# Expert lists cut to their likely length with the rest in runtime branches, and a new order and mix for the last layer

## The chip, the core and the metric

The kernel runs on one core of one Trainium2 chip. The metric is the device time of one execution in microseconds. Five engines work side by side and wait for each other by semaphores: TensorE (PE; its weight loads are shown as PEld), VectorE (DVE), ScalarE (ACT), GpSimd (POOL) and SyncE (SP). SP issues the plain transfers here, POOL the indirect ones, whose addresses are read from a table of row numbers.

## The reference

A model of four layers on x of shape [4, 1024, 128] in float32. Each layer is a token mixer and a feed-forward part, and after each of the eight a layer norm without gain:

```python
x = layernorm(x + L0_attn(x)); x = layernorm(x + L0_ffn(x))
x = layernorm(x + L1_attn(x)); x = layernorm(x + L1_ffn(x))   # 16 experts, 4 a token, and a shared one
x = layernorm(x + L2_attn(x)); x = layernorm(x + L2_ffn(x))   # 8 experts, 2 a token
x = layernorm(x + L3_attn(x)); x = layernorm(x + L3_ffn(x))   # 32 experts, 4 a token, and a shared one
```

The mixer of layer 3 is the one that the change touches. Its sequence axis is the axis of length 4 (the rows), so that the Toeplitz mix runs over four positions with seven coefficients a head:

```python
rms = norm(query, axis=-1) * 128 ** -0.5
x = query / (rms + 1e-8)
u = silu(x @ u_w.T + u_b);  v = silu(x @ v_w.T + v_b)          # 256 features each
y[i] = sum over j of toeplitz[i - j] * v[j]                    # i, j: the four rows
L3_attn = (u * y) @ o_w.T + o_b + query
```

A routed feed-forward part computes, for each token, the softmax or sigmoid of its router's logits, takes the best k experts, and adds their outputs with weights. An expert of layers 1 and 3 is `(silu(x @ gate) * (x @ up)) @ down` with 128 hidden units; one of layer 2 has 512 and low-rank additions.

## The kernel before

**Tokens and tiles.** The 4096 tokens lie in SBUF as `self.x`, 32 tiles of 128 tokens by 128 features. A quarter is 256 time steps of the four rows, 8 tiles. A `Part` is a set of tiles that goes through a stage together. In layer 1 part a has quarters 0 and 1, r quarters 2 and 3. In layer 2 part a has the same two quarters, m has rows 0 and 1 of quarters 2 and 3, n has their rows 2 and 3. In layer 3 part a has quarters 0 and 1, b quarter 2, c quarter 3.

**A routed part.** `positions` (L1231 to 1291) computes on VectorE and TensorE where each token's copies stand in a list that is sorted by expert, each expert's share padded to whole tiles of 128 rows. It leaves a table of row numbers `pos`, the weights `wk` and `ids`, the expert of each tile. `spread` (L1307, its transfers recorded at L1295) has POOL scatter the rows of x into a list in DRAM, one indirect transfer for each tile and choice. The list has room for the worst padding: the number of tiles times k, plus one for each expert, in whole groups of four: 80 tiles for layer 1's parts, 40, 24 and 24 for layer 2's a, m and n, 96, 64 and 64 for layer 3's a, b and c. Lists are zeroed at the start by SP (`zero_lists`, L1343).

**Experts.** `small_experts` (L1663; layers 1 and 3) and `l2_experts` (L1440) walk the whole list in groups of four tiles: `inputs` loads a group by SP and transposes it, `up` multiplies by gate and up, `turn` transposes the product, `down` multiplies by down, and SP stores the result into a second list, ys. Each group's experts are read from `ids` into registers of the engines (L1337). When the last group is issued, the name "made ..." goes into `self.listed`. `collect` (L1350) then has POOL gather k rows for each token from ys into a tile `yt`, and VectorE adds them into x with their weights (L1361). A gather waits for a free `yt`; in layer 3 the pool `yp` has 8 of them, each for one tile's four gathers.

**Layer 3's mixer.** `l3_attn` (L1512) works quarter by quarter: norm of 8 tiles (L185, applied on VectorE at L205), the root mean square by squares and sums (L1548, L1549), scaling, twice the input plus the bias put back into x (L1564), transposes, projections to u and v with `silu`, the mix over the rows, the output matmul and its sum with x, and a second norm. The mix is on VectorE: for each of 2 feature chunks and 4 rows one product (L1590), three multiply-adds (L1592) and a product with u (L1594 or L1596). With `exps` (part a) ScalarE is kept to the table that the layer-2 softmax uses; parts b and c go without.

**The order.** Every stage is a Python generator; what it issues between two `yield`s is a step. `mix(main, side, pace)` (L233) interleaves a main generator and a side one by the costs that the steps yield, written by hand. `abreast` (L1772) runs generators in turn, `chain` one after the other, `when` waits until a name is in `listed`, `press` runs the side until a condition holds. From the parts of layer 2 on, one side chain `on` runs through all stages (L1858 to 1887). Its last piece has, in order: the collection of n's rows, the mixer and routing of b, then b's scatter and `last(a, yp)` (64 gathers of a and its final norm) abreast with the mixer and routing of c, then c's scatter, and `last(b, yp)`. The main generators beside it are the shared expert and the experts of a, b and c. At the end `close(c, yp)` collects c. `last` (L1809) is `collect` and `finish` (L1738), which norms and stores the output.

After all that, one branch on `flag` (L1891, 1892) guards a general version of layer 2 and what follows, for inputs that overflow the fast softmax; with these inputs it isn't run.

Of the kernel before, what the change touches and what calls it, by code (L numbers as in the profile page):

```python
# [12 lines left out]
I32 = mybir.dt.int32  # L13
# [61 lines left out]
class Kernel:  # L75
# [109 lines left out]
    def norm(self, tiles, by="act"):  # L185

        nc, n = self.nc, len(tiles)
        mv = self.tile(self.small, [P, n, 2], f"mv{n}")
        for t, x in enumerate(tiles):
            st = self.tile(self.small, [P, 6], "bn")  # L190
            nc.vector.bn_stats(st, x)  # L191
            nc.vector.bn_aggr(mv[:, t, :], st)
        rstd = self.tile(self.small, [P, n], f"rstd{n}")
        if by == "act":
            nc.scalar.activation(rstd, mv[:, :, 1], AF.Sqrt, bias=self.eps)
            nc.vector.reciprocal(rstd, rstd)
        else:
            ve = self.tile(self.small, [P, n], f"ve{n}")
            nc.vector.tensor_scalar(ve, mv[:, :, 1], LN_EPS, None, ALU.add)
            if by == "pool":  # L200
                nc.gpsimd.tensor_tensor(rstd, ve, self.mhalf[:, :n], ALU.pow)
            else:
                self.rsqrt(rstd, ve)
        for t, x in enumerate(tiles):
            nc.vector.tensor_scalar(x, x, mv[:, t, 0:1], rstd[:, t : t + 1], ALU.subtract, ALU.mult)  # L205
# [1025 lines left out]
    def positions(self, cp, name, mask, w, nt, ne, k):  # L1231
# [51 lines left out]
        nc.vector.tensor_copy(ids, pe[0:1, :P])  # L1283

# [6 lines left out]
        self.route[name] = [pos, wk, ids, []]  # L1291
# [15 lines left out]
    def spread(self, lay, part, k):  # L1307

        pos, _, _, done = self.route[lay + part.name]
# [32 lines left out]

    def zero_lists(self, *lays):  # L1343

        for rows, _, tl in (v for k, v in self.lists.items() if k[0] in lays):
            self.nc.sync.dma_start(
                out=rows.rearrange("(t p) d -> p t d", p=P), in_=self.zero.unsqueeze(1).to_broadcast([P, tl, D])
            )

    def collect(self, lay, part, k, yp, first=0, nt=None):  # L1350

        nc = self.nc
        pos, wk, _, _ = self.route[lay + part.name]
# [12 lines left out]
        for t in range(first, first + (nt or part.nt)):  # L1366
# [73 lines left out]
    def l2_experts(self, part, wall):  # L1440
        nc = self.nc
        NC, EW = F2 // P, 3 * F2
        pos, wk, ids, done = self.route["l2" + part.name]
        rows, ys, tl = self.lists["l2", part.name]
        with ExitStack() as ctx:
# [47 lines left out]


# [3 lines left out]
            for n in range(tl + 1):  # L1498
# [8 lines left out]
                if n == tl:  # L1507
                    self.listed.add("made l2" + part.name)
# [3 lines left out]
    def l3_attn(self, part, exps=False):  # L1512
# [5 lines left out]
        with ExitStack() as ctx:  # L1518
# [19 lines left out]
            for q in range(part.q0, part.q0 + part.nq):  # L1538
                s = slice(q * QT, (q + 1) * QT)
                self.norm(self.quarter(q), by="dve" if exps else "act")  # L1540
                yield (7.0,)
                xq = self.tile(vp, [P, QC], "xq")
                rms = self.tile(self.small, [P, QT], "rms")
                for g in range(2):
                    sg = slice(q * QT + g * 4, q * QT + g * 4 + 4)
                    r = rms[:, g * 4 : g * 4 + 4]
                    sq = self.tile(vp, [P, 4, D], "sq")
                    nc.vector.tensor_tensor(sq, x[:, sg, :], x[:, sg, :], ALU.mult)  # L1548
                    nc.vector.tensor_reduce(r, sq, AX.X, ALU.add)  # L1549
                    if exps:  # L1550

                        ri = self.tile(self.small, [P, 4], "rmsi")
                        v = self.tile(self.small, [P, 4], "rmsv")
                        nc.vector.tensor_scalar(v, r, 1e-30, None, ALU.max)
                        self.rsqrt(ri, v)
                        nc.vector.tensor_tensor(r, r, ri, ALU.mult)
                    else:
                        nc.scalar.activation(r, r, AF.Sqrt)
                    nc.vector.tensor_scalar(r, r, float(np.float32(D ** -0.5)), 1e-8, ALU.mult, ALU.add)
                    nc.vector.reciprocal(r, r)  # L1560
                    yield (4.0,)
                    nc.vector.tensor_tensor(sq, x[:, sg, :], r.unsqueeze(2).to_broadcast([P, 4, D]), ALU.mult)

                    stt(  # L1564
                        x[:, sg, :], x[:, sg, :], 2.0, self.row["l3_ob"].unsqueeze(1).to_broadcast([P, 4, D]),
                        ALU.mult, ALU.add,
                    )
# [6 lines left out]
                for c in range(NC):  # L1574
                    v = self.tile(vp, [P, B, TQ], "v")
                    for i, dst in ((1, v), (0, u[:, c])):
                        for g in range(2):
# [3 lines left out]
                            yield (2.3,)  # L1581

                    cf = col["toep"][:, c * 7 : (c + 1) * 7]
                    for i in range(B):
                        y = self.tile(vp, [P, TQ], "y", bufs=1 if exps else 2)
# [7 lines left out]
                        if exps:  # L1593
                            stt(u[:, c, i, :], u[:, c, i, :], 0.25, y, ALU.mult, ALU.mult)  # L1594
                        else:
                            nc.vector.tensor_tensor(u[:, c, i, :], u[:, c, i, :], y, ALU.mult)  # L1596
                        yield (3.0,)
                for g in range(2):
                    py = self.tile(ps, [P, 4, D], "s")
                    for k in range(4):  # L1600
                        b, h = (g * 4 + k) // 2, k % 2
                        for c in range(NC):
                            self.mm(py[:, k, :], u[:, c, b, h * P : (h + 1) * P], wo[:, c, :], c == 0, c == NC - 1)
                    sg = slice(q * QT + g * 4, q * QT + g * 4 + 4)
                    nc.vector.tensor_tensor(x[:, sg, :], py, x[:, sg, :], ALU.add)
                    yield (3.0,)
                self.norm(self.quarter(q), by="dve" if exps else "act")
# [4 lines left out]


# [49 lines left out]
    def small_experts(self, lay, ne, part, wall):  # L1663

        nc = self.nc
        pos, wk, ids, done = self.route[lay + part.name]
        rows, ys, tl = self.lists[lay, part.name]
        with ExitStack() as ctx:
# [46 lines left out]


# [3 lines left out]
            for g in range(ng + 1):  # L1720
# [7 lines left out]
                if g == ng:  # L1728
                    self.listed.add(f"made {lay}{part.name}")
# [8 lines left out]
    def finish(self, part):  # L1738

        for q in range(part.q0, part.q0 + part.nq):  # L1740
            self.norm(self.quarter(q))
            yield (5.0,)
            for b in range(B):
                t = tile_of(b, 2 * q)
                self.nc.sync.dma_start(
                    out=self.out[b, q * TQ : (q + 1) * TQ, :].rearrange("(k p) d -> p k d", p=P),
                    in_=self.x[:, t : t + 2, :],
                )
            yield (1.0,)
# [59 lines left out]
    def last(self, part, yp):  # L1809
        yield from self.collect("l3", part, K3, yp)  # L1810
        yield from self.finish(part)
# [12 lines left out]
    def all(self):  # L1824
# [4 lines left out]
        with ExitStack() as ctx:  # L1829
# [36 lines left out]
            with ExitStack() as c3:  # L1866
                with ExitStack() as c2:
# [5 lines left out]
                    on = self.chain(on, self.rows_in(m2))  # L1873
                    self.run(self.mix(self.l2_experts(n2, wall), on, drain=False))
                self.press(on, listed("l3a"))
                yp = self.pool(c3, "l3y", 8)
                on = self.chain(
                    on, self.rows_in(n2), self.l3_attn(b), self.l3_route(b),
                    self.abreast(
                        self.chain(self.spread("l3", b, K3), self.when(listed("made l3a")), self.last(a, yp)),  # L1880
                        self.chain(self.l3_attn(c), self.l3_route(c)),
                    ),
                    self.spread("l3", c, K3), self.when(listed("made l3b")), self.last(b, yp),
# [8 lines left out]
        with self.tc.If(bad > 0):  # L1892
            with ExitStack() as ctx:
# [4 lines left out]
                for p in self.by_rows:  # L1898
# [3 lines left out]
                    self.run(self.rows_in(p))  # L1902
                for p in self.parts:
                    self.run(self.onward(p))
                    with ExitStack() as c2:
                        sw, wall = self.l3_wall(c2)
                        self.run(self.l3_shared(p, sw), self.l3_experts(p, wall))
                        self.run(self.last(p, self.pool(c2, "l3y" + p.name, 5)))
# [165 lines left out]
```

## Time and profile before

| what | us |
|---|---|
| median of three runs | 2526.44 (2516.18 to 2534.73) |
| the profiled execution | 2521.14 |
| its span | 2519.3 |

Where the stages of the last third stand in the profiled execution, by the instructions that open or close them:

| us from the start | what |
|---|---|
| 1720 to 1767 | experts of m (layer 2) on TensorE |
| 1787.3 | positions of a (layer 3) are there |
| 1788 to 1874 | POOL scatters a |
| 1943.5 | last experts of n (layer 2) |
| 1989 to 2102 | experts of a, with b's mixer and routing beside them |
| 2106.6 | positions of b |
| 2107 to 2148, 2148 to 2190 | POOL scatters b, gathers the first half of a's |
| 2205 to 2335 | experts of b |
| 2277.6 | positions of c |
| 2284 to 2326, 2338 to 2378 | POOL scatters c, gathers b's |
| 2385 to 2461 | experts of c |
| 2465 to 2505 | POOL gathers c's |
| 2519.3 | end |

The profile page gives, for each engine, its busy time as a share of the span; the span cut in 40 slices of 63 us with a digit for each; the chain of work that ended last; and groups of equal instructions. A group's line reads: line of the kernel, engine, operation, output tile <- input tiles, count, busy time in us, mean in ns, then the idle time before it and what ended that. Three groups of the mixer, for all calls of its kind:

```profile
L205 DVE TENSOR_SCALAR x<-x,mv,rstd 128x128 f32<-128x128 f32 x256 | 71.9, 354 | 4.0 <-POOL rstd L201 3.1
...
L1592 DVE SCALAR_TENSOR_TENSOR y<-v,ld,y 128x256 f32<-128x256 f32 x96 | 43.7, 480 | 7.1 <-ACT v L1531 5.6
...
L1590 DVE TENSOR_SCALAR y<-v,ld 128x256 f32<-128x256 f32 x32 | 10.5, 345 | 22.5 <-issue 22.4
```

96 instructions of the multiply-add took 43.7 us in all, 480 ns each, and VectorE sat idle 7.1 us before them.

### The profile page before, as it was taken

The numbers are of one execution on the slowest core, as the hardware profiler recorded it, in microseconds if no ns is written. First come the engines' busy times: TensorE is split into PE (matmuls) and PEld (weight loads), VectorE is DVE, ScalarE is ACT, GpSimd is POOL, SyncE is SP. The second block draws the span as 40 slices with busy tenths as digits, with TensorE's granted clock in tenths as the row PEclk, the third lists the DMA queues.
The fourth block names the chain that finished last, engine by engine and source line by source line (L and its number), as shares of the span: only waits on it lengthen the run. The fifth ranks groups of instructions, "written<-read, shape, count | busy, mean of one in ns | idle before, by whom it ended". The sixth has DMA issues, their size and how long they took to land.

```text
span 2519.3 us, 28678 instructions
## 1 busy us (share of the span) xinstructions
PE 1708.3 (68%) x9605; PEld 1036.4 (41%) x9605; DVE 1344.4 (53%) x3801; ACT 828.6 (33%) x1193; POOL 767.0 (30%) x701
## 2 busy tenths in 40 slices
PE   7535775985652864887888778978718896374490
PEld 3224333853320444755523232345415684163280
DVE  8857894656551643334536664654603575163363
ACT  5510471432320431222246554622202353131140
POOL 5521384136145004213231002001470204536404
PEclk9756788998775987898979898988958998587695
DMA  9900002334100032312210000030410232132242
GB/s 308 289 2 0 16 34 87 118 130 164 48 30 37 27 126 93 106 48 60 89 48 16 1 1 18 1 128 32 168 65 23 74 114 72 40 108 81 63 126 60
DMA packets 225735, 192.05 MB, mean 76 GB/s; under 512 B 17008, under 2 KB 204272, under 8 KB 225072
## 3 DMA queue, kind: packets, MB, share of 16 engines
q1 hardware_dynamic: 204880, 147.28, 18.4%
q0 software_dynamic: 20704, 42.86, 5.4%
q8 instruction: 83, 1.36, 0.2%
q14 instruction: 68, 0.56, 0.1%
HBM read 93.47 MB, written 96.60 MB: 75 GB/s over the span
## 4 chain that ended last, share of the span: by engine, by line
PE 36%; another core or an unknown queue 18%; DVE 14%; issue 4%; ACT 3%; POOL 2%; DMA 2%; SPq 0%; DVEq 0%; POOLq 0%; ACTq 0%
PE gu L157 10%; PE s L157 8%; PE sc L157 5%; PE yp L157 5%; PE tp L165 4%; ACT pr L1051 1%; DVE pr L1057 1%; POOL yt L1295 1%; DVE x L205 1%; PE pu L157 1%; PE py L157 1%; PE pg L157 1%; DVE x L1361 1%; DVE bn L191 1%
## 5 line engine op out<-in xcount | busy, mean ns | idle before, releaser
L1051 ACT ACTIVATE pr<-sc 128x1024 f32<-128x1024 f32 x288 | 279.6, 1021 | 326.3 <-PE sc L157 205.8
L157 PE MATMUL gu<-ld,xgT 128*128 x768 | 203.2, 408 | 69.0 <-ACT xgT L167 40.7
L157 PE MATMUL sc<-qm,kT 32*128 32x512 f32 (+3 forms) x1536 | 202.1, 566 | 11.9 <-ACT pr L1051 8.9
L157 PE MATMUL s<-pr,va 128*32 128x512 f32 (+3 forms) x1536 | 179.2, 537 | 44.7 <-issue 26.9
L157 PEld LDWEIGHTS gu<-ld,xgT 128*128 128x128 f32 x768 | 145.7, 201 | 98.3 <-ACT xgT L167 45.2
L165 PE MATMUL tp<-ld,hg 128*128 128x128 f32 x736 | 120.0, 286 | 94.1 <-issue 46.9
L157 PE MATMUL gu<-wall,xgT 128*128 x352 | 180.7, 639 | 2.8 <-ACT xgT L167 2.0
L169 DVE COPY hT<-tp 128x512 f32<-128x512 f32 x140 | 95.8, 685 | 128.4 <-PE tp L165 61.4
L165 PEld LDWEIGHTS tp<-ld,hg 128*128 128x128 f32 x736 | 95.2, 147 | 153.9 <-issue 86.2
L1693 DVE TENSOR_TENSOR hg<-sg,gu 128x256 f32<-128x256 f32 x192 | 78.7, 416 | 138.9 <-ACT sg L1692 117.9
L1057 DVE TENSOR_TENSOR pr<-pr,ld 128x512 f32<-128x512 f32 (+1 forms) x160 | 92.4, 580 | 104.4 <-ACT pr L1051 102.1
L1692 ACT ACTIVATE sg<-gu 128x256 f32<-128x256 f32 x192 | 72.7, 383 | 209.8 <-PE gu L157 97.2
L167 ACT COPY xgT<-tp 128x512 f32<-128x512 f32 x118 | 69.0, 586 | 201.3 <-PE tp L165 152.4
L157 PEld LDWEIGHTS sc<-qm,kT 32*128 32x128 f32 x1536 | 86.1, 199 | 118.2 <-issue 69.2
L1466 ACT ACTIVATE sg<-gu 128x512 f32<-128x512 f32 x88 | 52.4, 598 | 238.1 <-PE gu L157 136.2
L165 PE MATMUL tp<-ld,xg 128*128 128x128 f32 x472 | 78.7, 294 | 52.4 <-ACT hT L167 29.5
L1295 POOL DMA_INDIRECT l1ra<-x,posl1a x64 | 93.3, 1458 | 61.2 <-DVE posl1a L1272 42.0
L157 PE MATMUL yp<-ld,hT 128*128 x768 | 105.3, 281 | 4.1 <-issue 1.9
L1468 DVE TENSOR_TENSOR hg<-sg,gu 128x512 f32<-128x512 f32 x88 | 59.9, 681 | 88.1 <-ACT sg L1466 75.1
L1295 POOL DMA_INDIRECT yt<-l1yr,posl1r x64 | 60.7, 949 | 146.7 <-DVE x L1361 72.2
L157 PEld LDWEIGHTS s<-pr,va 128*32 128x32 f32 x1536 | 38.5, 113 | 154.5 <-issue 106.7
L157 PE MATMUL yp<-wall,hT 128*128 x704 | 98.3, 286 | 1.5 <-DVE hT L169 1.5
(433 smaller groups left out, 3543.4 us busy)
## 6 DMA issues: line engine op xcount, KB each, us to landing
wall<-wall SPq DMA_DIRECT2D x16, 768.0 KB
l3ra<-zero SPq DMA_DIRECT2D x1, 6144.0 KB
ld<-in_l_w SPq DMA_DIRECT2D x2, 3072.0 KB
wall<-we SPq DMA_DIRECT2D x24, 256.0 KB
ld<-in_l_w SPq DMA_DIRECT2D x1, 6144.0 KB
xg<-l3ra SPq DMA_DIRECT2D x24, 256.0 KB
l3ya<-yg SPq DMA_DIRECT2D x24, 256.0 KB
l1ra<-zero SPq DMA_DIRECT2D x1, 5120.0 KB
```

What stands on the lines that cost most here:

```text
L157: return self.nc.tensor.matmul(out, lhsT, rhs, start=start, stop=stop)
L165: nc.tensor.transpose(pt[:, k * P : (k + 1) * P], s, self.ident)
L167: nc.scalar.copy(dst, pt[:, : n * P])
L169: nc.vector.tensor_copy(dst, pt[:, : n * P])
L191: nc.vector.bn_stats(st, x)
L1051: nc.scalar.activation(pr, sc[h], AF.Exp)
L1057: nc.vector.tensor_tensor(d, d, cst["tril"].unsqueeze(1).unsqueeze(1).to_broadcast([P, 2, n, P]), ALU.mult)
L1295: ins = self.nc.gpsimd.indirect_dma_start(**kw)
L1466: nc.scalar.activation(sg, gu[:, 0, :], AF.Silu)
L1468: nc.vector.tensor_tensor(h, sg, gu[:, 1, :], ALU.mult)
L1692: nc.scalar.activation(sg, pg[:, :, 0, :], AF.Silu)
L1693: nc.vector.tensor_tensor(h[:, 2 * c : 2 * c + 2, :], sg, pg[:, :, 1, :], ALU.mult)
```

## The change

**Lists.** A new function `likely` gives a shorter length for each list (the tiles times k plus half the number of experts, in whole groups). The expert loops end there. What lies beyond, up to the full length, is put into a branch that every engine takes or skips by a count, `used`, which `positions` now also copies out. `zero_lists` also zeroes the part of ys that lies beyond.

```diff
+        used = self.tile(self.routes, [1, 1], f"used{name}", I32)
+        nc.vector.tensor_copy(used, end[0:1, ne - 1 : ne])
...
+    def likely(self, part, ne, k):
+        return -(-(part.nt * k + ne // 2) // 4) * 4
+
+    def rest_of(self, used, at, tl, body):
+        if at >= tl:
+            return
+        n = self.nc.values_load(used, min_val=0, max_val=tl, skip_runtime_bounds_check_because="a list's tiles")
+        with self.tc.If(n > at):
+            for g in range(at // 4, tl // 4):
+                body(g)
...
-        rows, ys, tl = self.lists[lay, part.name]
+        rows, ys, total = self.lists[lay, part.name]
+        tl = self.likely(part, ne, K3)
...
+            def rest(g):
+                inputs(g)
+                up(g)
+                turn(g)
+                down(g)
...
                 if g == ng:
+                    self.rest_of(used, tl, total, rest)
                     self.listed.add(f"made {lay}{part.name}")
```

The lengths become 72 and 72 (of 80) in layer 1, 36 (of 40), 20 and 20 (of 24) in layer 2, 80 (of 96), 48 and 48 (of 64) in layer 3.

**Layer 3's mixer.** The root mean square comes from the norm's own variance. The output bias is a matmul of one row into the output's PSUM tile. For b and c (no `exps`) the norm is applied on ScalarE, and the mix is a matmul with 14 diagonal matrices (7 coefficients, 2 chunks), made once by `l3_mixes`.

```diff
         for t, x in enumerate(tiles):
-            nc.vector.tensor_scalar(x, x, mv[:, t, 0:1], rstd[:, t : t + 1], ALU.subtract, ALU.mult)
+            if on_act:
+                nc.scalar.activation(x, x, AF.Identity, bias=off[:, t : t + 1], scale=rstd[:, t : t + 1])
+            else:
+                nc.vector.tensor_scalar(x, x, mv[:, t, 0:1], rstd[:, t : t + 1], ALU.subtract, ALU.mult)
...
-                    nc.vector.tensor_tensor(sq, x[:, sg, :], x[:, sg, :], ALU.mult)
-                    nc.vector.tensor_reduce(r, sq, AX.X, ALU.add)
...
-                    stt(
-                        x[:, sg, :], x[:, sg, :], 2.0, self.row["l3_ob"].unsqueeze(1).to_broadcast([P, 4, D]),
-                        ALU.mult, ALU.add,
-                    )
...
+                    if not exps:
+
+                        for i0 in range(0, B, 2):
+                            y = self.tile(ps, [P, 2, TQ], "s")
+                            lags = [0, -1, -2, -3, 1] if i0 == 0 else [0, 1, 2, 3, -1]
+                            for lag in lags:
+                                lo, hi = max(i0, lag), min(i0 + 2, B + lag)
+                                self.mm(
+                                    y[:, lo - i0 : hi - i0, :], self.mixes[:, c * 7 + (lag if lag >= 0 else 3 - lag), :],
+                                    v[:, lo - lag : hi - lag, :], lag == 0, lag == lags[-1],
+                                )
+                            nc.vector.tensor_tensor(u[:, c, i0 : i0 + 2, :], u[:, c, i0 : i0 + 2, :], y, ALU.mult)
+                            yield (4.5,)
+                        continue
...
+                        self.mm(py[:, k, :], self.cst["all1"][0:1, :], self.row["l3_ob"][0:1, :], True, False)
...
-                    nc.vector.tensor_tensor(x[:, sg, :], py, x[:, sg, :], ALU.add)
+                    stt(x[:, sg, :], x[:, sg, :], 2.0, py, ALU.mult, ALU.add)
...
+        for k in range(14):
+            self.nc.vector.tensor_scalar(self.mixes[:, k, :], self.ident, self.col["toep"][:, k : k + 1], None, ALU.mult)
```

**Order.** n's rows are gathered in two halves, quarter 2's tiles first; b's mixer and routing run abreast with the second half. The last gathers of a go in two quarters: the first beside c's mixer, the second behind c's scatter.

```diff
                 on = self.chain(
-                    on, self.rows_in(n2), self.l3_attn(b), self.l3_route(b),
+                    on, self.collect("l2", n2, K2, yp, which=(0, 1, 4, 5)),
                     self.abreast(
-                        self.chain(self.spread("l3", b, K3), self.when(listed("made l3a")), self.last(a, yp)),
+                        self.chain(self.l3_attn(b), self.l3_route(b)),
+                        self.collect("l2", n2, K2, yp, which=(2, 3, 6, 7)),
+                    ),
+                    self.abreast(
+                        self.chain(self.spread("l3", b, K3), self.when(listed("made l3a")), self.last(a, yp, 0)),
                         self.chain(self.l3_attn(c), self.l3_route(c)),
                     ),
-                    self.spread("l3", c, K3), self.when(listed("made l3b")), self.last(b, yp),
+                    self.spread("l3", c, K3), self.last(a, yp, 1), self.when(listed("made l3b")), self.last(b, yp),
                 )
```

## The prediction

> **What bounds the kernel now.** I read the busy shares first, then the chain of waits, then a table of stretches and the timelines inside them.
>
> ```profile
> PE 1708.3 (68%) x9605; PEld 1036.4 (41%) x9605; DVE 1344.4 (53%) x3801; ACT 828.6 (33%) x1193; POOL 767.0 (30%) x701
> ...
> PEclk9756788998775987898979898988958998587695
> ...
> GB/s 308 289 2 0 16 34 87 118 130 164 48 30 37 27 126 93 106 48 60 89 48 16 1 1 18 1 128 32 168 65 23 74 114 72 40 108 81 63 126 60
> ...
> PE 36%; another core or an unknown queue 18%; DVE 14%; issue 4%; ACT 3%; POOL 2%; DMA 2%; SPq 0%; DVEq 0%; POOLq 0%; ACTq 0%
> ```
>
> TensorE (PE) is the longest engine and carries 36% of the chain, but 18% is a wait that the profile cannot name. The chain shows where it sits:
>
> ```profile
> 749.25 59.20 another core or an unknown queue
> ...
> 2348.13 35.59 another core or an unknown queue
> ```
>
> and PE's own timeline shows what it is:
>
> ```profile
> 757.31 0.80 PE L157 MATMUL s<-pr,va 128*32 128x384 f32 x1 [1.31 <-issue]
> 760.11 0.80 PE L157 MATMUL s<-pr,va 128*32 128x384 f32 x1 [2.00 <-issue]
> 762.90 0.37 PE L157 MATMUL s<-pr,va 128*32 128x128 f32 x1 [2.00 <-issue]
> ```
>
> Nothing holds these matmuls, yet one starts every 2.8 us. Both stretches lie in an unbroken run of POOL's indirect transfers (718 to 799: layer 1's scatter; 2338 to 2378: gathers of b). The same shows in every such run, from some 13 to 20 us after it began until it ends. I call it the crawl. The last stages, by stretch (sum and mean lines left out):
>
> ```profile
> core 0: us, PE busy (x) PEld busy (x) DVE busy (x) ACT busy (x) POOL busy (x), PEclk, DMA share, GB/s
> ...
> 1989.00:2107.00 118.00, 108.97 (x673) 92.60 (x673) 89.37 (x285) 62.21 (x114) 0.00 (x0) 0.99 0.37 111
> 2128.00:2196.00 68.00, 14.10 (x19) 4.37 (x20) 11.57 (x28) 5.81 (x8) 45.59 (x48) 0.55 0.16 47
> 2196.00:2278.00 82.00, 64.09 (x372) 54.17 (x370) 50.38 (x180) 28.02 (x54) 26.49 (x28) 0.89 0.35 100
> ...
> 2385.00:2462.00 77.00, 69.38 (x422) 59.70 (x422) 43.58 (x117) 31.27 (x62) 0.00 (x0) 0.94 0.38 114
> 2462.00:2519.00 57.00, 0.00 (x0) 0.00 (x0) 16.91 (x60) 1.35 (x5) 30.24 (x32) 0.50 0.19 52
> ```
>
> PE bounds the experts of a (109 of 118 us) and of c (69 of 77); the crawl empties 2128 to 2196 (19 matmuls); the end waits for POOL's last gathers.
>
> [...] Before has one branch (L1892):
>
> ```profile
> L1892 PEldq COMPARE_BRANCH  x1: 4333/4333/4333, 2460.3 to 2460.3; - x1
> L1892 ACTq COMPARE_BRANCH  x1: 50/50/50, 2510.7 to 2510.7; - x1
> ```
>
> [...]
>
> **The change part by part.**
>
> Ends of lists. 19 groups of four tiles move into branches. Counting the reference's own routing of its inputs, the eight lists need 71, 72, 36, 20, 20, 78, 45 and 46 tiles of the 72, 72, 36, 20, 20, 80, 48 and 48 that stay outside: no body runs. On PE a group of layers 1 and 3 repeats every 3.5 us (starts at 2405.8, 2409.6, 2413.1), one of layer 2 takes 12.5 (four tiles at 3.05 to 3.5; PE is busy all of 1720 to 1767). Layer 1: 4 x 3.5 = 14; layer 2: 3 x 12.5 = 37.5; layer 3: 12 x 3.5 = 42. PE's busy shares there (layer 1: 85 of 99 us; layer 2: 47 of 47) say 51.5 of layers 1 and 2 lie on the path.
>
> Price of a skipped body: a register load, 0.33 to 0.62 us by the rows of before, and the branch, 0.06 to 4.3: between 0.5 and 5. A gain is excluded: it only adds instructions. [...] I take 3.5, five times in layers 1 and 2: 17.5. Net -34.
>
> Zeros. 76 tiles x 64 KB = 5 MB more on SP's queue; at the 308 GB/s of the first slice 16 us, in front of two slices that move 2 and 0. Cost 0, hidden by them; if they were full, up to 16. The `used` copies and the 14 diagonal tiles (14 x 0.354, the norm's 128x128 row) fall where VectorE has room (43 busy of 67 us in 1720 to 1787): 0, at most 5.
>
> Attention of layer 3. Per quarter of b and c VectorE loses 8 x (0.345 + 3 x 0.480 + 0.419) = 17.6 of mix, 16 norm applications x 0.354 = 5.7 to ScalarE, and 4.1 of squares, sums and bias; it gains 4 x 0.68 = 2.7: net -24.7. PE gains 12 matmuls of 512 columns at 0.86 (the projections' spacing outside the crawl), 8 of 256 at half of it, 8 of 128 at 0.29: +16. ScalarE's 128x128 form is not in the trace: 0.3 to 0.586 (its 128x512 copy) each, 16 of them 5 to 9 us, where 54 of 82 are free: 0. Part a, two quarters beside layer 2's experts: VectorE -8, PE +4.6; I take 0, -8 to +5.
> In 1989 to 2107 (b's attention beside a's experts) PE is the bound: -14 for four groups, +16 for b, branch +3.5, and the branch sits on VectorE inside b's positions: +3.5, less some of VectorE's 24.7 in that chain: take +4 (0 to +9). Half of n's gathers (8 x 1.26 = 10 us, 0.95 busy and 0.30 between) no longer precede b's attention; shared a fills PE then, so take -4 of 10.
>
> So b's positions, at 2106.6 before, come at 2106.6 - 34 + 4 - 4 = 2073. Call it T; before has 2519.3 - 2106.6 = 413 us after it.
>
> The tail. Scatter of b and a's first gathers, 64 x 1.26 = 81 us, crawl as now (T+20 to T+83). Then attention c. Its 82 us (2196 to 2278) have PE 64 and VectorE 50 busy; VectorE loses 25 and 32 adds (x 0.34 = 11), PE gains 16 and loses some groups of b; POOL is quiet. I take the same chain a little shorter: c's positions at T+165 (T+171 before). Then POOL runs c's scatter (T+206), a's second quarter (T+247) and b's gathers (T+288), with pauses only where the 8 buffers of `yp` wait for VectorE's adds. If a pause ends the crawl, experts c start about T+247; if not, T+288. They take 12 groups at 77/16 = 4.8: 58, then branch 4, gathers c 40, adds and norm 14: 116 in all. End T+363 to T+404, against T+413: -9 to -50. I take -26 and say so: nearer the unbroken run. The number of transfers is equal; a's second 32 gathers, its adds and SP's four stores of that quarter now stand behind c's scatter, and b's gathers wait behind them; c's stay last.
>
> Sum: -34 + 4 - 4 - 26 = -60. The profiled run took 2521.1 (span 2519.3 and 1.8), so 2461; it lies 5.3 below the median of the runs, 2526.4, to which 2465 answers.
>
> **The rivals.**
> 1. The likeliest: groups pay, branches are cheap, the tail gains some: 2465, own range 2440 to 2490. For it: PE's shares. Chance 0.54.
> 2. The branches cost 5 and the tail's crawl eats its gain: -51.5 + 25 + 5 - 4 - 5 = -30: 2496. For it: 4.33 us on PE. 0.16.
> 3. Each branch some 10 us [...] and the tail -9: -51.5 + 50 + 9 - 4 - 9 = -5: 2521. For it: every engine has one; against it: no all-engine barrier. 0.14.
> 4. Slower: [...] PE waits as in the crawl. Without branches the sum is -60 - 17.5 - 3.5 - 4 = -85 over seven branches on the path; it turns at 12 us each. At 17 it is +34: 2560. For it: the crawl's cause is unknown; against it: a list's gathers start only after its branch. 0.16.
> That the change does not do what it says, a list passing its limit by rounding, would run one body, 7 to 14 us: inside rival 1.
>
> **How the numbers follow.** A measurement tells 1% (25 us) from no change: faster is below 2501, slower above 2552. Faster: 0.54 and 0.13 of rival 2's: 0.67. Same: 0.17, slower 0.16. Range: low, branches at 0.5 (-49), all ten of the gathers and the tail's -50 with b's +4: -105, so 2421; I take 2425. High: rival 3 and part of 4, 2545.
>
> **What would show it.** In the changed profile: 99 register loads of groups instead of 118; PE's gap across each branch (3.5 taken, 12 decides); the crawl's spans, and whether one run of transfers reaches from c's scatter to b's gathers; c's positions 165 us after b's; VectorE's busy sum lower by more than 58 (2 x 25 + 8), PE's by about 52 (93.5 - 32 - 9). Wrong if a body runs, a gap is over 10 us, or experts c begin later than T+288.

## The result, and the profile after

| | before | after |
|---|---|---|
| median of 20 runs, us | 2530.9 (2513.99 to 2540.22) | 2508.0 (2495.75 to 2521.55) |
| span of the profiled execution, us | 2519.3 | 2503.8 |

The ratio is 0.9921 with a 95% interval of 0.9901 to 0.9941: a gain of 0.8%, some 20 us. Forecast was 2465, or 61 us less than the median of before that it started from (its sum of -60 makes 2466). The time lies in the range, but the gain is a third of the forecast. Three lines of the page of after (engine busy sums, granted clock by slices, bytes moved by slices):

```profile
PE 1661.2 (66%) x9161; PEld 987.2 (39%) x9161; DVE 1260.3 (50%) x3586; ACT 793.2 (32%) x1138; POOL 768.6 (31%) x701
...
PEclk9766788997865977898899988979759998595785
...
GB/s 309 287 86 0 17 34 96 110 133 157 38 35 40 20 139 89 86 59 57 113 20 1 1 1 18 1 134 39 175 40 30 91 68 55 36 101 56 55 95 67
```

TensorE's sum fell by 47 us (52 forecast) and VectorE's by 84 (over 58 forecast): the work left as planned. TensorE has 99 register loads of groups instead of 118, so that no body of a branch ran. The larger zeroing shows in the third slice, 86 GB/s where before had 2, and nothing waits for it: the first experts of layer 1 start 6 us earlier than before (433.6 against 439.5). The chain of waits of after reaches back over the last 60 us alone, so that no share stands beside the 18% of before. Sums say nothing of where the time went; a table of the same events in both traces does. This one has the three kernels between before and after as well (they are the first three experiments below; "order" is the new order of the gathers). All times are us from the start of the profiled execution.

| event | before | lists alone | lists and mixer | lists and order | after |
|---|---|---|---|---|---|
| n's last register load of experts (layer 2) | 1925.8 | 1878.2 | 1883.0 | 1875.6 | 1882.4 |
| a's first one (layer 3) | 1992.8 | 1948.2 | 1951.6 | 1957.5 | 1961.5 |
| a's last one | 2092.6 | 2027.0 | 2049.9 | 2043.0 | 2069.8 |
| b's positions (POOL's scatter of b starts within 1 us) | 2106.6 | 2068.6 | 2081.0 | 2069.7 | 2087.5 |
| last sum of b's shared expert | 2204.8 | 2111.4 | 2173.6 | 2134.5 | 2191.9 |
| c's positions | 2277.6 | 2227.8 | 2232.4 | 2228.7 | 2242.8 |
| c's first register load | 2398.7 | 2336.8 | 2373.5 | 2332.1 | 2365.0 |
| last store of c's experts | 2460.9 | 2385.2 | 2420.5 | 2413.3 | 2444.1 |
| end | 2519.3 | 2444.4 | 2480.1 | 2471.7 | 2503.8 |

After is 43 us ahead of before at the last experts of n, 31 at a's first group, 19 at b's positions, 35 at c's positions and 15 at the end. So the lists paid more than forecast, and three places gave it back: the shared part of a, the experts of a, and the tail.

**The shared part of a.** After's timeline of POOL and VectorE:

```profile
1908.43 0.69 DVE L744 TENSOR_TENSOR hs<-sg,pu 128x512 f32<-128x512 f32 x1 [1.03 <-PE pg L157]
...
1923.04 0.95 POOL L1305 DMA_INDIRECT yt<-l2yn,posl2n  x1 [0.30 <-issue]
1924.14 0.69 DVE L1709 TENSOR_TENSOR x<-py,x 128x512 f32<-128x512 f32 x1 [15.02 <-DMA yt<-l2yn,posl2n]
```

n's gathers now use `yp`, whose 8 buffers hold both halves, so 16 transfers run from 1904.3 to 1924.0 without a break. The sum at L1709 waits 15 us although the matmuls that it needs are recorded at 1909.7 to 1912.8; it starts 0.15 us after POOL's run ends. The view names the gather that landed last, but the instruction itself waits for TensorE, whose signal for these matmuls the trace has at 1924.1; the one before came at 1909.9. So by its signals TensorE was held for 14 of the run's 20 us, although the records of these matmuls stand 11 us ahead of the signal. Before, these gathers waited for adds and had breaks of up to 8 us.

**The experts of a.** TensorE in two stretches of after, and the new matmuls of the stage by groups:

```profile
1990.00:2048.00 58.00, 58.00 (x302) 43.93 (x302) 19.90 (x40) 19.46 (x38) 0.00 (x0) 1.00 0.26 78
2048.00:2077.00 29.00, 24.76 (x156) 21.23 (x155) 18.45 (x89) 25.00 (x47) 0.00 (x0) 0.94 0.19 58
```

```profile
L157 PE MATMUL s<-v,mixes 128*128 128x512 f32 x24 | 11.0, 592 | 0.0
L210 ACT ACTIVATE x<-x,off,rstd 128x128 f32<-128x128 f32 x24 | 9.8, 482 | 0.9 <-DVE off L207 0.9
...
L157 PE MATMUL s<-v,mixes 128*128 128x256 f32 x16 | 4.1, 379 | 0.0
L157 PE MATMUL s<-rows,ld 1*128 1x128 f32 x16 | 3.9, 321 | 0.0
```

The columns of a stretch are its length and then busy time of PE, its weight loads, VectorE, ScalarE, POOL. TensorE has no free time from 1990 to 2048 while VectorE is 34% busy. Mix and bias take 11.0 + 4.1 + 3.9 = 19 us (16 forecast; there are two records to each of the 12, 8 and 8 matmuls). In the second stretch ScalarE, which now applies the norm, is as full as TensorE (25 of 29 us each).

**The tail.** Four stretches of after:

```profile
2262.00:2322.00 60.00, 8.26 (x32) 6.32 (x32) 3.56 (x8) 1.35 (x3) 45.55 (x48) 0.56 0.19 57
2338.00:2400.00 62.00, 51.67 (x272) 39.13 (x272) 24.02 (x53) 17.64 (x36) 7.57 (x8) 0.95 0.29 82
2400.00:2430.00 30.00, 14.14 (x72) 12.37 (x72) 12.14 (x46) 2.71 (x6) 22.85 (x24) 0.76 0.28 74
2449.50:2495.00 45.50, 0.00 (x0) 0.00 (x0) 21.23 (x79) 1.19 (x4) 30.57 (x32) 0.50 0.26 67
```

In the first one POOL scatters c and gathers a's second quarter, and TensorE gets 32 matmuls in 60 us; the last of b's experts stand in it, and their last store comes at 2337.4. b's gathers don't start then, but 48 us later:

```profile
2385.89 0.95 POOL L1305 DMA_INDIRECT yt<-l3yb,posl3b  x1 [61.52 <-DVE x L1396]
```

The 8 buffers of `yp` hold a's second quarter, gathered by 2324. VectorE frees them by its adds (L1396), and in its order of instructions these stand behind c's shared part and the first experts of c: the first of them runs at 2383.8. So b's gathers (2386 to 2430) lie over the experts of c, where TensorE is busy 14 of the 30 us from 2400. Twelve groups of c take 79 us (2365.0 to 2444.1), where lists alone take 48 (2336.8 to 2385.2). In the three kernels of the table that gather a in one piece (before, lists alone, lists and mixer) the gathers of b are over before c's experts start.

**The branches.** All eight of them on three of the engines:

```profile
L1363 POOLq COMPARE_BRANCH  x8: 45/45/57, 491.9 to 2388.4; - x8
L1363 PEldq COMPARE_BRANCH  x8: 215/338/352, 510.4 to 2443.5; - x8
L1363 ACTq COMPARE_BRANCH  x8: 45/45/50, 512.2 to 2443.8; - x8
```

The three numbers are shortest, median and longest in ns. On VectorE and SyncE the longest takes 72 and 53 ns. None comes near the 4.33 us that the one branch of before takes on TensorE; the same branch takes 4.62 us there in after.

### The profile page after: what moved, and what is told of

Its sections match the earlier page's. It is cut to its first block, busy times and chain, and to the rows that moved or that the text cites. A ratio compares the mean times of both kernels' runs of the same rounds, so it can differ in the third digit from the quotient of the medians.

```text
span 2503.8 us, 27293 instructions
## 1 busy us (share of the span) xinstructions
PE 1661.2 (66%) x9161; PEld 987.2 (39%) x9161; DVE 1260.3 (50%) x3586; ACT 793.2 (32%) x1138; POOL 768.6 (31%) x701
## 5 line engine op out<-in xcount | busy, mean ns | idle before, releaser
L157 PE MATMUL gu<-ld,xgT 128*128 x640 | 172.6, 414 | 91.0 <-issue 51.8
L157 PEld LDWEIGHTS gu<-ld,xgT 128*128 128x128 f32 x640 | 124.1, 205 | 118.7 <-issue 65.9
L165 PE MATMUL tp<-ld,hg 128*128 128x128 f32 x624 | 102.7, 286 | 99.2 <-issue 50.4
L157 PE MATMUL gu<-wall,xgT 128*128 x304 | 157.1, 643 | 2.1 <-ACT xgT L167 2.0
L169 DVE COPY hT<-tp 128x512 f32<-128x512 f32 x118 | 81.0, 686 | 149.3 <-remote 79.0
L165 PEld LDWEIGHTS tp<-ld,hg 128*128 128x128 f32 x624 | 80.5, 147 | 153.1 <-issue 84.4
L1752 DVE TENSOR_TENSOR hg<-sg,gu 128x256 f32<-128x256 f32 x160 | 66.0, 416 | 146.4 <-ACT sg L1751 124.0
L165 PE MATMUL tp<-ld,xg 128*128 128x128 f32 x396 | 64.7, 290 | 67.8 <-issue 41.9
L157 PE MATMUL yp<-ld,hT 128*128 x640 | 88.3, 282 | 24.7 <-DVE hT L169 24.0
L1305 POOL DMA_INDIRECT l1rr<-x,posl1r x64 | 62.2, 972 | 99.9 <-DVE posl1r L1280 80.8
```

Of the source, the lines that this page charges most:

```text
L157: return self.nc.tensor.matmul(out, lhsT, rhs, start=start, stop=stop)
L165: nc.tensor.transpose(pt[:, k * P : (k + 1) * P], s, self.ident)
L169: nc.vector.tensor_copy(dst, pt[:, : n * P])
L1305: ins = self.nc.gpsimd.indirect_dma_start(**kw)
L1752: nc.vector.tensor_tensor(h[:, 2 * c : 2 * c + 2, :], sg, pg[:, :, 1, :], ALU.mult)
```

## The experiments

Kernels that stand together were timed beside the kernel before on one chip; ratios are to that. The wait that I call the crawl was the suspect from the start, but first the parts were taken apart.

### Which part gives it back

`lists_only` is after with the old mixer, norm and order of `on`. `no_order` and `no_mixer` revert one of the two:

```diff
-                    self.spread("l3", c, K3), self.last(a, yp, 1), self.when(listed("made l3b")), self.last(b, yp),
+                    self.spread("l3", c, K3), self.when(listed("made l3b")), self.last(b, yp),
...
-                on = self.chain(on, self.l3_mixes(c3), self.rows_in(m2))
+                on = self.chain(on, self.rows_in(m2))
```

> Only the ends of the lists go into branches; mixer and order are those of before. Theory A (the lists pay as the changed trace shows upstream, -43 us at the last experts of n, and the new mixer and order give it back): -43, four groups less for a (-14 + 3 for the branch) and four for c (-16 + 4): -66, 2465 us (2450 to 2480). Rival B ([...] mixer and order are harmless): as the changed kernel, 2500 to 2510.

> The changed kernel with the old order of gathers (n's rows all at once ahead of b's mixer, a's 64 gathers beside c's mixer). Theory A: the 15 us stall of VectorE in the shared part of a is gone (-12), experts of c no longer run under b's gathers (-17): about 2480 us. Rival B: within 8 us of the changed kernel's 2508. Rival C (the new mixer on TensorE alone eats the gain): within 8 us of 2508 too, and no_mixer far below.

> The changed kernel with the old mixer of layer 3 (mix on VectorE, norm applied on VectorE, squares and sums). Theory A: experts of a are bound by TensorE and lose 19 us of mixing matmuls, c's positions come some 7 later: 2490 to 2500 us. Rival C: about 2470. Rival B: within 8 us of 2508.

| kernel | median, us | ratio | interval |
|---|---|---|---|
| lists_only | 2438.5 | 0.9643 | 0.9588 to 0.9698 |
| no_order (lists, mixer) | 2491.9 | 0.9869 | 0.9807 to 0.9932 |
| no_mixer (lists, order) | 2464.7 | 0.9739 | 0.9681 to 0.9797 |

The lists alone bring 88 us, more than expected (2438.5 lies under 2450 to 2480); the mixer costs 53 of them, the order 26; together they cost 70 (0.9921 - 0.9643 = 0.028). `no_mixer` falls where rival C, the mixer, had put it. The mixer's cost is nearly three times its matmuls. The register loads of the experts show what happens (the last two times are the first and the last load). The traces hold 36 of the 53 us (spans of 2444.4 and 2480.1), as the profiled run of `lists_only` was the slowest of its four and that of `no_order` the fastest. `lists_only` first, then `no_order`:

```profile
L1339 PEldq TENSOR_LOAD <-idsl3a x20: 327/332/588, 1948.2 to 2027.0; - x20
...
L1339 PEldq TENSOR_LOAD <-idsl3b x12: 328/331/640, 2116.2 to 2219.9; - x12
L1339 PEldq TENSOR_LOAD <-idsl3c x12: 328/334/437, 2336.8 to 2376.3; - x12
```

```profile
L1347 PEldq TENSOR_LOAD <-idsl3a x20: 328/332/592, 1951.6 to 2049.9; - x20
...
L1347 PEldq TENSOR_LOAD <-idsl3b x12: 327/332/616, 2180.2 to 2260.1; - x12
L1347 PEldq TENSOR_LOAD <-idsl3c x12: 327/331/537, 2373.5 to 2411.7; - x12
```

With the mixer the experts of a take 98 us instead of 79: that is the 19 us of matmuls. But b's start moves by 64. Between the end of a's experts and POOL's next run lies time for b's shared expert: a's last store to b's first scatter takes 29.4 us in `lists_only` and 19.4 in `no_order`. In the first the shared part is done 1.4 us after the scatter (2111.4), in the second the run catches it, and it ends at 2173.6. Its output matmuls, first and last start, in `lists_only` and then in `no_order`:

```profile
L157 PE MATMUL py<-ld,hs x64: 272/275/377, 2057.8 to 2075.0; 128*128 128x128 f32 x64
```

```profile
L157 PE MATMUL py<-ld,hs x64: 273/275/275, 2077.2 to 2173.3; 128*128 128x128 f32 x64
```

The first kernel issues them all within 6 us of the scatter's start at 2069.1, the second starts them 5 us before its scatter at 2082.0. In after that gap is 11.3 us and in before 5; in both the shared part ends some 60 us after the scatter. The gap is also all that the four groups taken from a's experts leave: b's positions, whose routing follows the last group, don't come sooner after a's first load (120 us in `lists_only`, 114 before).

### The branches

`no_branch` drops register loads, compares and bodies:

```diff
-        n = self.nc.values_load(used, min_val=0, max_val=tl, skip_runtime_bounds_check_because="a list's tiles")
-        with self.tc.If(n > at):
...
+        return
```

> The changed kernel without the branches: what lies beyond the shorter lists is left out altogether, [...] with these inputs nothing of the result lies there. Theory A, by the gaps of 1.2 to 4.2 us on TensorE across seven branches: 15 to 25 us less, 2485 to 2493. Rival B [...]: 40 us less or more, under 2470.

2503.3 us, 0.9904 (0.9876 to 0.9933), against after's 0.9921 (0.9901 to 0.9941). Eight branches cost some 4 us together, half a microsecond each, and the intervals include nothing. The expectation of 15 to 25 was too high, and the rival's 40, by which the branches had eaten the gain, is out.

### The two parts, cut finer

`a_split` is `lists_only` with a's second quarter gathered behind c's scatter, but n's rows as before. `mix_only` is `no_order` with the norm back on VectorE:

```diff
-                self.norm(self.quarter(q), by="dve" if exps else "act", on_act=not exps)
+                self.norm(self.quarter(q), by="dve" if exps else "act")
```

> lists_only (2438 us) with one part of the new order: a's last gathers in two quarters, the second behind c's scatter; n's rows are gathered as before. Theory A (the loss of the order lies in the tail, where b's gathers now run beside the experts of c): 2465 us, as no_mixer, with the last store of c's experts some 28 us later against their last register load. Rival (it lies in n's unbroken run of 16 gathers, which stalls VectorE for 15 us in the shared part of a): 2438 to 2446.

> lists_only with the new mixer, except that the norm of b and c is still applied on VectorE. Theory A (the mixing and bias matmuls lengthen the stage of a's experts, which TensorE bounds, by some 19 us, and b's experts then start inside the scatter and gathers instead of ahead of them): within 8 us of no_order, 2484 to 2500, and b's first list load at 2170 or later. Rival (the norm on ScalarE, 16 x 0.48 us with table loads beside the experts' activations, is what costs): 2438 to 2455.

`a_split` took 2458.0 (0.9709, 0.9671 to 0.9748): 0.7% over `lists_only`, so most of the order's 1.0% lies in the tail, though the intervals overlap. Its last store of c's experts comes 32 us after their last load (2367.3 to 2399.4; 28 expected), against 9 in `lists_only`. As in after, b's gathers wait for the adds of a's second quarter: they start at 2341.7, though b's experts had stored their last at 2225.0, so that it isn't b's experts that hold them. `mix_only` took 2496.1 (0.9847, 0.9797 to 0.9896), as `no_order`: where the norm is applied makes no difference that shows. What is left of the new mixer takes work from VectorE and adds the 19 us of mix and bias to TensorE, which leaves these matmuls as the cost.

### Is the crawl the cause?

If the losses are TensorE's work falling into unbroken runs of indirect transfers, breaks in the runs should return them. `paced` is `lists_only` with two memsets after each of the 640 transfers, `paced8` has sixteen after each eighth:

```diff
+        self.pause = self.tile(self.const, [P, 256], "pause")
...
         self.moved = self.moved[-130:] + [ins.ins.name]
+        self.nth += 1
+        if self.nth % 1 == 0:
+            for _ in range(2):
+                p = self.nc.gpsimd.memset(self.pause, 0.0)
+                self.tc.add_manual_dep(p.ins, self.moved[-1], behind, reason="queued behind")
+                self.moved.append(p.ins.name)
```

> lists_only with two POOL memsets of 128x256 (about 0.3 us each) after every indirect transfer, 640 times; the order of everything else is kept. Theory P (TensorE's crawl comes of unbroken runs; at 6 transfers in 10 us or less the traces show none): the stretches of more than 1.4 us a matmul vanish, the runs last 1.5 times as long, the last gathers cost 19 us more: 2300 to 2420 us. Rival Q (each transfer stops TensorE for its own time, whatever the gap, or the crawl has nothing to do with POOL): 2470 to 2560, and the unnamed wait stays.

> lists_only with 16 such memsets after every eighth transfer: runs of 8 (10 us) and pauses of some 5 us; the same POOL time as paced. Theory P with the 13 to 20 us that a run needs before TensorE slows: as paced or better, 2280 to 2420. If it's the mean rate that matters and not the run: as paced. If the pause must come after every transfer: 2440 or more, with crawl inside each run.

`paced` took 2252.8 us, 0.8891 (0.8853 to 0.8929), and `paced8` 2395.9, 0.9473 (0.9435 to 0.9512). The memsets of `paced` keep POOL busy for 413 us more, and the kernel is 185 us faster than `lists_only`, more than expected. The stretch of layer 1's scatter of r, its 64 transfers and little more, in `lists_only` and then in `paced`:

```profile
714.00:794.00 80.00, 18.52 (x96) 6.87 (x96) 14.67 (x52) 3.98 (x4) 60.55 (x63) 0.59 0.13 51
```

```profile
731.00:851.00 120.00, 93.34 (x859) 47.41 (x859) 83.80 (x222) 50.41 (x52) 105.78 (x190) 0.94 0.13 49
```

96 matmuls in 80 us became 859 in 120, with the same transfers at 1.82 us instead of 1.26 apart. Theory P holds for `paced`. `paced8` has no crawl in this scatter either (777 matmuls in 123 us), but gains only 43 us over `lists_only`, inside the 2280 to 2420 expected but far from `paced`; which of its runs of eight still crawl was not settled.

Not every standstill under a run is the crawl. In b's scatter `paced` passes 60 matmuls and `lists_only` 56. There VectorE's sum of b's shared part waits until the scatter has read the rows that it is about to change, and the rest of VectorE's work waits behind it:

```profile
1890.16 0.69 DVE L1704 TENSOR_TENSOR x<-py,x 128x512 f32<-128x512 f32 x1 [16.83 <-DMA l3rb<-x,posl3b]
```

In `lists_only` the same wait is 12.7 us: pauses lengthen it.

### Do mixer and order still cost when the crawl is gone?

The same pauses were put into after (`after_paced`), `no_order` and `no_mixer`; `paced_half` is `lists_only` with one memset.

> The changed kernel with the same pauses as paced (two memsets after every indirect transfer). Theory A+P (mixer and order lose mostly because more TensorE work falls into unbroken runs): it gains more than lists_only did (185 us), 2508 - 240 = 2268 us (2250 to 2290). Rival R (their losses of 53 and 26 us are TensorE work and waits that pauses don't touch): 2253 + 70 = 2323.

> Lists and the new mixer, old order, with the same pauses. A+P: what is left of the mixer's loss is the 19 us of matmuls in the stage that TensorE bounds, less what VectorE gains in c's mixer: 2260 to 2275 us. Rival R: 2253 + 53 = 2306.

> Lists and the new order, old mixer, with the same pauses. A+P: b's gathers beside the experts of c no longer slow them; the order costs nothing or gains a little: 2240 to 2258 us. Rival R: 2253 + 26 = 2279.

> lists_only with one memset (0.32 us) after every transfer instead of two: the interval goes from 1.26 to some 1.5 us. If a gap of any size is enough: 2230 to 2250 (less POOL time than paced at the end). If the interval has to pass some 1.6 us: 2380 to 2438, crawl in the trace. In between if TensorE gets a share in proportion to the gap: about 2340.

On the chip of these four the kernel before took 2098.1 us (2095.5 to 2101.6), not 2527: the wait seems to be missing there. The ratios were 1.0638 (1.0618 to 1.0659) for `after_paced`, 1.0800 (1.0771 to 1.0829) for `no_order_paced`, 1.0638 (1.0618 to 1.0659) for `no_mixer_paced` and 1.0084 (1.0062 to 1.0106) for `paced_half`. Among each other they can be compared: with pauses and the new order, the mixer costs nothing, and the new order gains 1.5% on top of the mixer. Against before, the three with two memsets lose 6 to 8% there. So the question was put again, with unpaced kernels beside paced ones:

> The changed kernel itself beside before. If before takes about 2527 here: 2508, as known. If before takes about 2098 (no crawl), theory A+P: the lists bring some -60 to -70, the mixer's matmuls +19 in a's stage, the order and c's lighter mixer -10 to -40: 2000 to 2050 us, a clear gain over before. Rival R (mixer and order cost 70 us whatever the crawl): 2080 to 2095.

> Lists alone. With before at 2527: 2438, as known. With before at 2098, A+P: 2020 to 2040, within 25 us of after_u, and not 70 below it. Rival R: 2010 to 2025, 70 below after_u.

> Lists with one memset after each transfer (interval 1.46 us). With before at 2527: if a gap of any size ends the crawl about 2115, as in the last call; if not, 2250 to 2438. With before at 2098: 2114, and above lists_u, since pauses only cost there.

> The changed kernel with two memsets after each transfer (interval 1.82). With before at 2527, A+P: within 25 us of paced (2253), as in the last call (2233), since the crawl is gone in both; rival R: 2323. With before at 2098: 2233 again, some 200 above after_u: there the pauses have nothing to remove.

This chip had the wait (before at 2514.3):

| kernel | pause | interval of transfers, us | median, us | ratio | interval |
|---|---|---|---|---|---|
| after_u | none | 1.26 | 2487.5 | 0.9906 | 0.9875 to 0.9938 |
| lists_u | none | 1.26 | 2428.7 | 0.9663 | 0.9629 to 0.9697 |
| after_paced_u | two memsets | 1.82 | 2240.6 | 0.8923 | 0.8891 to 0.8955 |
| half_u | one memset | 1.46 | 2185.2 | 0.8706 | 0.8677 to 0.8735 |

Without pauses after lies 59 us over the lists alone. With two memsets it lies at 0.8923, and the lists (`paced`, on another chip with the wait) at 0.8891: the two intervals overlap, and what is left is some 8 us. So with pauses 50 to 60 of the 59 to 70 us that mixer and order cost no longer show.

That doesn't yet say that the crawl was their cause, for the pauses have made POOL the bound. Two stretches from b's positions on, `paced` up to the end of b's gathers, then `after_paced_u` up to the end of c's:

```profile
1860.00:2160.00 300.00, 147.03 (x730) 110.72 (x729) 125.15 (x405) 60.06 (x113) 259.67 (x480) 0.73 0.26 78
```

```profile
1861.00:2223.00 362.00, 176.89 (x898) 133.82 (x896) 138.26 (x443) 71.47 (x134) 309.56 (x575) 0.75 0.27 77
```

In both POOL makes no break of over 1.5 us, and TensorE is busy half the time. A delay of TensorE can hide there, whatever caused it. In `no_mixer_paced`, for one, b's positions come 13 us sooner than in `after_paced` (1847.6 and 1860.6), and POOL then stands 14 us for c's positions. That the crawl is what the mixer runs into rests on the traces without pauses: b's shared expert, ahead of the run in `lists_only` and inside it in `no_order`.

Two of the kernels ran on both kinds of chip, and tell how much of the wait is left. After with two memsets takes 2240.6 us here and 2233.1 on the chip without the wait; the lists with one take 2185.2 (`half_u`) and 2114.5 (`paced_half`). In the scatter of r `half_u` passes 563 matmuls in 95 us and `paced_half` 711 in 96. So an interval of 1.46 us is not quite enough to end the crawl. `half_u` is nevertheless the best version by far on such a chip, 13% under before.

The last two asked for the smallest pause, and ran on a chip without the wait (before at 2101.5):

> The changed kernel with one memset of 128x256 after every transfer. With before at about 2520: A+P: within 25 us of half_u, a ratio to before of 0.862 to 0.880. Rival R (mixer and order cost 70 us by themselves): 0.898. With before at about 2098: above 2098 times 0.99, since pauses only cost there.

> lists_only with one memset of 128x4 (0.1 us) after every transfer. With before at about 2520: if it is enough that any other instruction of POOL stands between two transfers: 0.84 to 0.875. If the interval decides (1.26 us crawls, 1.46 hardly): 0.90 to 0.966. With before at about 2098: 0.97 to 1.0, as lists_only would be there.

`after_half` took 2098.9, 0.9991 (0.9979 to 1.0004), `paced_tiny` 2062.4, 0.9818 (0.9776 to 0.9860). The tiny memset fits into the 0.30 us between transfers (interval 1.27), so `paced_tiny` is almost `lists_only` there: its scatter of r passes 646 matmuls in 85 us without any real pause. On such a chip no slowing of TensorE shows even at 1.27 us, and lists bring about 39 us, not 88. `after_half` lies 0.9% under `paced_half` of the other such chip (0.9991 against 1.0084): mixer and order together gain there, with a pause.

What stays open: why two of the five chips of the experiments don't show the wait, what of POOL's transfers holds TensorE on the others, whether the tiny memset would be enough on those, and what after itself takes without pauses on a chip without the wait; none of these was run. No `lists_only` with two memsets was timed on a chip without it either. And no run keeps POOL from being the bound while it ends the crawl, so how much of the mixer's 53 us is the crawl stays an argument from the traces.

## Why the prediction was wrong

**Ends of lists: right in kind, too small.** The net of -34 upstream was -43 in after and -48 with lists alone, at n's last register load. The groups were sized right; a skipped body was priced at 3.5 us, the author's estimate between 0.5 and 5, and costs about half a microsecond. The one branch of before sits ahead of a long body, and its 4.33 us on TensorE was the wrong row to lean on; the lower bound of 0.5 was the answer. Alone the lists bring 88 us; by the trace b's shared expert then ends ahead of the crawl, 93 us sooner than before.

**Zeros, `used`, diagonals: right.** Nothing of them shows on the path.

**The step that failed first: the stage of a's experts at +4, with -4 for n's gathers.** From n's last load to b's positions nothing was to change; it took 205 us in after and 181 before, +24. The matmuls were sized well (+16 forecast, 19 measured). The three other terms were wrong. The -14 of the four groups was taken off the way to b's positions, because TensorE is the fullest engine of the stage; with lists alone b's positions come no sooner after a's first load (120 us against 114), and what the groups leave is time for b's shared expert. Using up that time was priced at nothing: POOL's run starts at b's positions whatever TensorE has left over, and 19 us of matmuls cost 53 by the end. And "shared a fills PE then" was taken for a cover of n's gathers, when their new buffers made an unbroken run of 16 that held TensorE from its sixth microsecond on, and the shared part lost 12 us instead of gaining 4.

**The step that failed second: the tail at -26, and in it the length of the pause before b's gathers.** From b's positions to the end it took 416.3 us, 413 before: +3. c's positions came at T+155 (T+165 forecast) and c's first group at T+278 (forecast T+247 to T+288). The forecast then gave 12 groups 58 us; they took 79. It named the cause itself, "pauses only where the 8 buffers of `yp` wait for VectorE's adds", and gave these pauses no length. One of them was 61.5 us, since the adds of a's second quarter stood behind c's shared part and first experts, and so the gathers of b fell on c's experts and slowed them. The forecast had watched how long a run is, and not where VectorE's order would let the next one start.

That the time lies in the stated range is luck: the range was wide for the sake of dear branches, which didn't come. Upstream was 9 us better than forecast, the two steps 24 and 29 us worse.

**The rivals.** The second had the right kind in one half, a tail whose crawl eats its gain, and the wrong half for the rest (branches at 5). The third and the fourth, 10 us and more at each branch, didn't happen: the eight together cost some 4 us.

## What to carry to other kernels

Where one kind of transfer slows an engine, the price of work on that engine isn't its duration but whether it ends before the transfers begin (19 us of matmuls cost 53 here): measure that gap first, and cost an edit against it. A buffer is free when the engine that empties it gets to it in its own order, not when the data are there (the gathers of b waited 61.5 us for that): look up what stands ahead of it. Take a price for a branch from one with a body of like length: on TensorE the branches over one to four groups took 0.22 to 0.35 us, the one over the general version 4.33 and 4.62; that the length makes the difference was not shown. And before fine edits around an unnamed wait, break up what runs under it once: two idle instructions after each transfer told more than any of the parts of this change; they can also make another engine the bound and so hide what is looked for, and the same kernels should be timed on another chip before such a wait is designed around.

## What the runs showed of the hardware

While POOL issues indirect transfers every 1.26 us without a break, TensorE is recorded in before to start one matmul in 2.8 us (757.31, 760.11, 762.90), and in layer 1's scatter 96 in 80 us in `lists_only`; at 1.82 us it runs on there (`paced`, 859 in 120 us). With one memset of 0.32 us after each transfer the lists went from 0.9663 to 0.8706 of before. Three of the five chips of the experiments showed this, with the kernel before at 2514 to 2531 us. On the two others it took 2098 and 2101 us, some 17% less, and 646 matmuls start in 85 us of that scatter at 1.27 us (`paced_tiny`). The page shows the wait as "another core or an unknown queue", with a granted clock of 0.50 to 0.60 in its stretches. What holds TensorE in it, no run here shows.
